# Cross-attention and a block-quantised feed-forward layer on one core: layer-norm scalings and the block-rounding additions moved from VectorE to GpSimd, with the rounding of 1024 columns cut into two halves

## The chip, the cores and the metric

The kernel runs on one core of a Trainium2 chip. The metric is the device time of one execution in microseconds (us). A core has several engines, each of which works through its own queue of instructions in order: TensorE (PE in the profile; its weight loads are shown apart as PEld), VectorE (DVE), ScalarE (ACT), GpSimd (POOL) and SyncE (SP), which issues most DMA transfers. Engines wait for each other through semaphores. SBUF is the on-chip memory, PSUM the small memory into which TensorE writes its products.

## The reference

There are B = 4 batches of N = 1024 rows of width 256, and 77 rows of context per batch. Cut to what matters:

```
# attention: 16 heads of width 16; keys are the 77 context rows and then the 1024 own rows
xn   = layernorm(x)
q    = xn @ Wq
k, v = split(concat(ctx, xn) @ Wkv)
dots = q k^T * 16 ** -0.5, causal over the own keys
x    = x + softmax(dots) v @ Wout + bout

# feed-forward: 256 -> 1024 -> 256, both factors of each product rounded in blocks of 32
def block_quant(v):                       # 3 mantissa bits
    amax  = max(abs(v)) over blocks of 32 along the last axis
    scale = 2 ** (floor(log2(amax)) - 3)
    return round(v / scale) * scale
h = gelu(block_quant(layernorm(x)) @ block_quant(w_fc)^T + b_fc)
x = x + block_quant(h) @ block_quant(w_proj)^T + b_proj
```

The kernel rounds a block by adding a large number `mag`, made from the block's largest magnitude, and subtracting it again: the addition in 32-bit floating point drops the bits that are to go. So a rounding is a maximum per block, two small operations that make `mag`, an add and a subtract.

## The kernel before, in words

Rows are handled in tiles of 128: eight tiles (`it`) per batch, 32 in all (`t`).

**The main loop.** Attention is cut into 16 parts, counted by `kk`: four batches times four groups of four heads. Each `kk` has 14 pieces (a piece is a stretch of up to 512 queries against 128 keys), each done in two half-steps of two heads. `half_step` (L831) issues, for two heads, two matmuls for the running maximum of the *next* `kk` (L451, into the PSUM tiles `s_ps`) and two matmuls for the scores of this one (L515, into `st_ps`); then VectorE reduces the two maxima (a plain reduce at L475 or a masked one with a running maximum at L477), ScalarE takes the exponential into an SBUF tile `pt` (L526) and GpSimd sets the masked part of the diagonal pieces to zero in place (`affine_select`, L531). The product with the values, `times_v` (L552), is issued two steps later. PSUM has three buffers for `s_ps` and two for `st_ps`; there are six `pt`.

**Everything else is fitted between half-steps.** A "unit" is a list of stages. `run` (L849) holds a list of units for each `kk`, with a price for each, and after each half-step begins as many as its budget allows, if their `ready` conditions hold. A unit's first stage is issued at once; each later one is issued a number of ticks after the one before it (a tick is a half-step): `LATER = 3`, unless the stage is given with a number of its own, as `(1, rounding)` is. The units that this change touches or that stand beside them:

- `norm_unit` (L304): `scale_rows` (L311) applies the first layer norm to a tile, `xh = (xn - mean) * rstd`; three ticks later PE transposes it (L324) and ScalarE copies it out (L326). There are 32. The roots `rstd` are made by `inv_std` (L153 to L163), 14 small VectorE operations for four tiles. The eight tiles of the first batch are done before the main loop starts.
- `in_unit` (L667): `quantize` applies the second layer norm (L674) to a tile `xh` of 256 columns and rounds it to `xq` (`quant_steps`, L171 to L180, and `quant_round`, L191 and L192); three ticks later PE transposes `xq` (L683). There are 32.
- `hidden_unit` (L694): matmuls to 1024 columns and the gelu on ScalarE (L713), into one of four buffers `h`.
- `out_unit` (L721): `largest` makes `mag` for the 1024 columns of `h`; one tick later `rounding` adds and subtracts, into one of two buffers `hq`; three ticks later `turn` transposes (L736) and ScalarE copies (L739); three more later `project` multiplies (L744), adds to `x` (L748) and issues the output transfer. `done["round"]`, counted in `rounding`, tells when the `h` buffer is free for another `hidden_unit`.
- `weight_unit` (L756): fetches and rounds a 128 x 256 block of a feed-forward weight. There are 16, in the first four `kk`.
- `clear_units` (L246): sets buffers to constants, on GpSimd: `vaug` (L248, L254), `qT` (L250) and `kT` (L252). They are issued after the norms of the first batch.

The feed-forward layer of a batch runs between the half-steps of the next batch: `in_unit`s in its second `kk`, `out_unit`s in the third and fourth. The last batch has no next one: from about 1084 us on, its feed-forward units are issued tick after tick with nothing beside them.

Before the change, the two steps of a rounding are on two engines:

```
nc.vector.tensor_tensor(src3, src3, magb, ALU.add)
nc.gpsimd.tensor_tensor(
    dst.rearrange("p (n k) -> p n k", k=QBLK), src3, magb, ALU.subtract
)
```

Of the kernel before, what the change touches and what calls it, by code (L numbers as in the profile page):

```python
# [10 lines left out]
BF16 = mybir.dt.bfloat16  # L11
I32 = mybir.dt.int32
AF = mybir.ActivationFunctionType
ALU = mybir.AluOpType
# [3 lines left out]
P = 128  # L18
# [10 lines left out]
QBLK = 32  # L29
# [14 lines left out]
def kernel(  # L44
# [14 lines left out]
    nc = tc.nc  # L59
    B, N, D = x.shape  # L60
    M = mem.shape[1]
    HID = w_fc.shape[0]
# [102 lines left out]
    def quant_steps(src, n, tag):  # L165

        nb = n // QBLK
        amax = small.tile([P, nb], F32, name=f"amax{tag}")  # L170
        nc.vector.tensor_reduce(  # L171
            amax, src.rearrange("p (n k) -> p n k", k=QBLK), axis=AX.X, op=ALU.max,
            apply_absolute_value=True,
        )
        mag = small.tile([P, nb], F32, name=f"mag{tag}")
        nc.vector.tensor_scalar(
            mag.bitcast(I32), amax.bitcast(I32), 0x7F800000, 0x00400000,
            ALU.bitwise_and, ALU.bitwise_or,
        )
        nc.vector.tensor_scalar(  # L180
            mag, mag, 1.5 * 2.0 ** -126, 2.0 ** (23 - MBITS), ALU.max, ALU.mult
        )
        return mag

    def quant_round(src, mag, dst):


        n = src.shape[-1]
        magb = mag.unsqueeze(2).broadcast_to([P, n // QBLK, QBLK])
        src3 = src.rearrange("p (n k) -> p n k", k=QBLK)  # L190
        nc.vector.tensor_tensor(src3, src3, magb, ALU.add)  # L191
        nc.gpsimd.tensor_tensor(  # L192
            dst.rearrange("p (n k) -> p n k", k=QBLK), src3, magb, ALU.subtract
        )
# [8 lines left out]
    with ExitStack() as actx:  # L203
# [11 lines left out]
        ffn = ap("ffn", 2)  # L215
# [40 lines left out]
        def s_tile(shape, dtype=F32):  # L256
            return ps_s.tile(shape, dtype, tag="s", name="s_ps")
# [11 lines left out]
        def cost(us, unit):  # L269

            first = unit[0] if isinstance(unit, list) else unit
            first.cost = us
            return unit
# [5 lines left out]
        def room(tag, bufs):  # L279
            return lambda: held[tag] < bufs  # L280
# [23 lines left out]
        def norm_unit(b, it):  # L304
            t = b * NT + it
            got = {}

            def scale_rows():
                held["xh"] += 1
                xh = work.tile([P, D], F32, name="xh")  # L310
                nc.vector.tensor_scalar(  # L311
                    xh, xn[b, it // HN][:, it % HN, :], mv1[:, t, 0:1], rstd1[:, t : t + 1],
                    ALU.subtract, ALU.mult,
                )
                got["xh"] = xh

            def turn():
                if it == 0:

                    assert b == 0 or projected[b - 1] == 2 * KC  # L320
                    xT[b] = xtp.tile([P, KC, KEYS], F32, name="xT")
                tp = s_tile([P, KC, P])
                for k in range(KC):
                    nc.tensor.transpose(tp[:, k, :], got["xh"][:, k * P : (k + 1) * P], ident)  # L324
                held["xh"] -= 1
                nc.scalar.copy(xT[b][:, :, M + it * P : M + (it + 1) * P], tp)  # L326
                normed[b] += 1

            scale_rows.ready = room("xh", XH)
            return cost(0.8, [scale_rows, turn])  # L330
# [256 lines left out]
        done = {"out": 0, "round": 0, "wout": 0, "begun": 0}  # L587
# [70 lines left out]
        xqT, hs, rooted = {}, {}, set()  # L658
# [8 lines left out]
        def in_unit(t):  # L667
            got = {}

            def quantize():  # L670
                done["begun"] += 1
                held["xq"] += 1
                xh = work.tile([P, D], F32, name="xh")
                nc.vector.tensor_scalar(  # L674
                    xh, x2[t], mv2[:, t, 0:1], rstd2[:, t : t + 1], ALU.subtract, ALU.mult
                )
                got["xq"] = ffn.tile([P, D], BF16, name="xq", bufs=XQ)
                quant_round(xh, quant_steps(xh, D, "x"), got["xq"])

            def turn():  # L680
                tp = s_tile([P, KC, P], BF16)
                for k in range(KC):
                    nc.tensor.transpose(tp[:, k, :], got["xq"][:, k * P : (k + 1) * P], identb)  # L683
                held["xq"] -= 1
                xqT[t] = ffn.tile([P, KC, P], BF16, name="xqT", bufs=HBUF + 1)
                nc.scalar.copy(xqT[t], tp)  # L686

            quantize.ready = lambda: (
                t // HN in rooted and done["begun"] - len(hs) <= HBUF
                and held["xq"] < XQ and held["xh"] < XH  # L690
            )
            return cost(1.6, [quantize, turn])
# [28 lines left out]
        def out_unit(t):  # L721
            got = {}

            def largest():
                held["hq"] += 1
                got["mag"] = quant_steps(hs[t], HID, "h")

            def rounding():
                got["hq"] = ffn.tile([P, HID], BF16, name="hq")
                quant_round(hs[t], got["mag"], got["hq"])  # L730
                done["round"] += 1

            def turn():
                tp = s_tile([P, HC, P], BF16)
                for k in range(HC):
                    nc.tensor.transpose(tp[:, k, :], got["hq"][:, k * P : (k + 1) * P], identb)  # L736
                held["hq"] -= 1
                got["hT"] = ffn.tile([P, HC, P], BF16, name="hT")
                nc.scalar.copy(got["hT"], tp)  # L739

            def project():
                yp = s_tile([P, D])
                for k in range(HC):
                    nc.tensor.matmul(  # L744
                        yp, got["hT"][:, k, :], wprT[:, k, :], start=(k == 0), stop=False
                    )
                nc.tensor.matmul(yp, ones3, bias3[:, B_PROJ : B_PROJ + D], start=False, stop=True)  # L747
                nc.vector.tensor_add(x2[t], x2[t], yp)  # L748
                nc.sync.dma_start(out=of[t * P : (t + 1) * P, :], in_=x2[t])
                done["out"] += 1  # L750

            largest.ready = lambda: t in hs and held["hq"] < 2
            return cost(4.4, [largest, (1, rounding), turn, project])


        def weight_unit(src, into):  # L756
# [144 lines left out]
        for kk in range(last + 1):  # L901
# [26 lines left out]
            else:  # L928
                n = -(-len(w_units) // NG)
# [61 lines left out]
```

## Time and profile before

| | |
|---|---|
| time, median of 4 runs | 1172.04 us (1169.41 to 1177.0) |
| the profiled execution | 1173.21 us, of which the profile's span is 1171.5 us |
| PE busy | 1043.7 us, 89% of the span |
| DVE busy | 767.8 us, 66% |
| ACT busy | 515.9 us, 44% |
| POOL busy | 224.8 us, 19% |
| TensorE clock granted, mean | 0.90 of full speed |

How to read the lines. The page gives busy time of each engine with its share of the span and its number of instructions; then the span in 40 equal slices, one digit for each: the busy share of the slice in tenths, and for PEclk the TensorE clock that was granted, in tenths of full speed; then the chain of work that ended last, by engine. A line of a group of instructions has the code line, the engine, the operation, what it writes and reads with shapes, how often it ran; after the first bar the total busy time in us and the mean of one in ns; after the second bar the idle time of the engine just before these instructions, and who ended it. A line of the timeline has the start in us, the duration in us and the operation; in square brackets the wait before it and who ended it.

### The profile page before, as it was taken

What the parts mean: (1) busy time and instruction counts of PE and PEld (TensorE: products, weight loads), DVE (VectorE), ACT (ScalarE), POOL (GpSimd) and SP (SyncE); (2) the same over time, 40 slices, a digit from 0 to 9 for tenths busy, and PEclk for the clock granted to TensorE, in tenths of its full rate; (3) what the DMA queues carried; (4) which work ended last, traced back from release to release, by engine and by line L of the source; (5) the groups of instructions that cost most, each with busy time, mean ns of one, the idle gap of its engine ahead of it and who ended that gap; (6) DMA issues with size and microseconds to landing.
All of it is one profiled execution on the core that took longest, in us unless ns stands there. A gap on an engine that the chain in (4) does not pass through costs nothing.

```text
span 1171.5 us, 20970 instructions
## 1 busy us (share of the span) xinstructions
PE 1043.7 (89%) x8014; PEld 432.2 (37%) x8024; DVE 767.8 (66%) x2410; ACT 515.9 (44%) x720; POOL 224.8 (19%) x419
## 2 busy tenths in 40 slices
PE   2799999999998899999988899999999899998665
PEld 1353334343433234344433324434434234343222
DVE  8686876665676575567568756657667586652654
ACT  2133554555343344565424364555434454663212
POOL 3000212121101122122201112112211122141312
PEclk9887999999978689999979689999999898999565
DMA  2121001101310001100320001010111000002100
GB/s 75 39 67 25 18 26 36 39 16 37 98 36 14 6 1 35 35 7 29 93 51 13 14 7 30 16 25 22 49 46 43 6 12 11 16 22 64 31 13 18
DMA packets 36118, 36.35 MB, mean 31 GB/s; under 512 B 14005, under 2 KB 29679, under 8 KB 36018
## 3 DMA queue, kind: packets, MB, share of 16 engines
q1 hardware_dynamic: 34912, 33.95, 10.6%
q8 instruction: 63, 1.03, 0.4%
q10 hardware_dynamic: 1106, 1.07, 0.3%
q14 instruction: 37, 0.30, 0.1%
HBM read 16.59 MB, written 5.24 MB: 19 GB/s over the span
## 4 chain that ended last, share of the span: by engine, by line
PE 68%; DVE 22%; issue 3%; DMA 2%; ACT 2%; SPq 1%; POOL 1%; POOLq 0%; DVEq 0%; ACTq 0%
PE s_ps L451 30%; PE av_ps L552 13%; PE s_ps L386 5%; DVE jk L477 4%; PE st_ps L515 4%; PE st_ps L702 3%; DVE mx L475 3%; PE s_ps L642 3%; DVE amaxh L171 2%; PE s_ps L359 2%; PE st_ps L707 2%; PE s_ps L744 2%; DVE h L191 1%; PE s_ps L736 1%; DVE st L145 1%
## 5 line engine op out<-in xcount | busy, mean ns | idle before, releaser
L451 PE MATMUL s_ps<-kT,qT 32*128 32x512 f32 (+2 forms) x1736 | 530.9, 566 | 59.3 <-DVE mxp L477 26.5
L526 ACT ACTIVATE pt<-st_ps 128x1024 f32<-128x1024 f32 (+4 forms) x448 | 355.4, 795 | 417.5 <-PE st_ps L515 392.1
L515 PE MATMUL st_ps<-qT,kT 32*128 32x512 f32 (+5 forms) x1792 | 533.6, 562 | 0.2 <-ACT pt L526 0.2
L451 PEld LDWEIGHTS s_ps<-kT,qT 32*128 32x128 f32 x1736 | 205.6, 195 | 252.7 <-DVE mxp L477 72.1
L531 POOL TENSOR_SCALAR_AFFINE_SELECT pt<-pt 128x254 f32<-128x254 f32 (+3 forms) x320 | 123.7, 388 | 618.3 <-ACT pt L526 618.3
L477 DVE CUSTOM_DVE_ANT_0 jk<-s_ps,tri,mx 128x77 bf16<-128x77 f32 (+3 forms) x372 | 173.1, 505 | 98.1 <-PE st_ps L515 73.1
L552 PE MATMUL av_ps<-pt,vaug 128*32 128x256 f32 (+7 forms) x3072 | 230.6, 374 | 7.2 <-POOL pt L531 4.2
L475 DVE TENSOR_REDUCE mx<-s_ps 128x1 f32<-128x512 f32 x248 | 159.7, 685 | 117.2 <-PE st_ps L515 94.0
L515 PEld LDWEIGHTS st_ps<-qT,kT 32*128 32x128 f32 (+1 forms) x1792 | 202.1, 191 | 14.7 <-issue 9.2
L477 DVE CUSTOM_DVE_ANT_0 jk<-s_ps,tri 128x512 bf16<-128x512 f32 (+3 forms) x248 | 126.6, 549 | 62.3 <-PE st_ps L515 50.4
L552 PEld LDWEIGHTS av_ps<-pt,vaug 128*32 128x32 f32 (+1 forms) x3072 | 62.3, 110 | 216.5 <-issue 167.5
L192 POOL TENSOR_TENSOR hq<-h,magh 128x1024 bf16<-128x1024 f32 x32 | 61.2, 1913 | 185.4 <-DVE h L191 185.4
L393 ACT COPY qk_st<-s_ps 128x512 f32<-128x512 f32 (+1 forms) x40 | 20.4, 514 | 73.2 <-PE s_ps L386 66.8
L713 ACT ACTIVATE h<-st_ps 128x1024 f32<-128x1024 f32 x32 | 32.8, 1024 | 39.9 <-PE st_ps L707 39.7
L702 PE MATMUL st_ps<-wfcT,xqT 128*128 128x512 bf16 x118 | 46.6, 477 | 4.2 <-ACT xqT L686 3.1
L739 ACT COPY hT<-s_ps 128x1024 bf16<-128x1024 bf16 x32 | 32.4, 1011 | 36.0 <-PE s_ps L736 35.8
L748 DVE TENSOR_TENSOR x<-x,s_ps 128x256 f32<-128x256 f32 x32 | 13.3, 416 | 47.8 <-PE s_ps L747 47.8
L642 PE MATMUL s_ps<-wo_sb,o_pk 128*128 128x256 f32 x128 | 41.6, 452 | 1.9 <-DVE o_pk L620 1.6
L171 DVE TENSOR_REDUCE amaxh<-h 128x32 f32<-128x1024 f32 x32 | 38.6, 1208 | 5.7 <-ACT h L713 5.7
L477 DVE DVE_READ_ACCUMULATOR2_ANT mxp<- 128x1 f32 x512 | 42.2, 82 | 0.0
L744 PE MATMUL s_ps<-wprT,hT 128*128 128x256 bf16 x256 | 40.5, 311 | 1.2 <-ACT hT L739 1.2
L191 DVE TENSOR_TENSOR h<-h,magh 128x1024 f32<-128x1024 f32 x32 | 39.4, 1233 | 0.4
(90 smaller groups left out, 766.5 us busy)
## 6 DMA issues: line engine op xcount, KB each, us to landing
kT<-qk_st SPq DMA_DIRECT2D x16, 275.2 KB
xn<-in_x_dram SPq DMA_DIRECT2D x16, 256.0 KB
qT<-qk_st SPq DMA_DIRECT2D x16, 256.0 KB
o_pk<-o_st SPq DMA_DIRECT2D x32, 128.0 KB
rb<-rd SPq DMA_DIRECT2D x128, 32.0 KB
x<-in_x_dram SPq DMA_DIRECT2D x32, 128.0 KB
out_dram<-x SPq DMA_DIRECT2D x32, 128.0 KB
x<-in_L_ffn_w_fc_dram SPq DMA_DIRECT2D x8, 128.0 KB
```

What stands on the lines that cost most here:

```text
L171: nc.vector.tensor_reduce(amax, src.rearrange("p (n k) -> p n k", k=QBLK), axis=AX.X, op=ALU.max, apply_absolute_value=True,)
L192: nc.gpsimd.tensor_tensor(dst.rearrange("p (n k) -> p n k", k=QBLK), src3, magb, ALU.subtract)
L451: nc.tensor.matmul(sp[:, 0 : hi - lo], qTs[kk % NQK][rows, it * P : (it + 1) * P], kTs[kk % NQK][rows, lo:hi], start=True, stop=True,)
L475: nc.vector.tensor_reduce(into, sp[:, 0:w], axis=AX.X, op=ALU.max)
L477: nc.vector.tensor_tensor_reduce(junk.tile([P, ICW], BF16, name="jk")[:, 0:w], sp[:, 0:w], mask, 1.0, before, ALU.add, ALU.max, into)
L515: nc.tensor.matmul(st[:nj, e, : i1 - i0], kTs[kk % NQK][rows, t * P : t * P + nj], qTs[kk % NQK][rows, i0:i1], start=True, stop=True,)
L526: nc.scalar.activation(pt[:nj, :, :w], st[:nj, :, :w], AF.Exp, scale=scale)
L531: nc.gpsimd.affine_select(out=pt[:nj, :, :behind], in_=pt[:nj, :, :behind], compare_op=ALU.is_ge, fill=0.0, base=base, pattern=[[0, 2], [1 ...
L552: nc.tensor.matmul(acc[c * PAD : (c + 1) * PAD, off + lo : off + hi], vaugs[b % 2][:nj, t, v0 : v0 + PAD], pts[kk, n, c // 2][:nj, c % 2, ...
L642: nc.tensor.matmul(yp, o_pk[b, ic][:, k, it * P % ICW : it * P % ICW + P], wo_sb[:, k, :], start=(k == 0), stop=False,)
L702: nc.tensor.matmul(hp[:, n, :], xqT[t][:, k, :], wfcT[:, k, n * ICW : (n + 1) * ICW], start=(k == 0), stop=False,)
L744: nc.tensor.matmul(yp, got["hT"][:, k, :], wprT[:, k, :], start=(k == 0), stop=False)
```

## The change

Three things move from VectorE to GpSimd, and one stage is cut in two.

1. The add of every rounding (`quant_round`, L191): 48 of 128 x 256 and 32 of 128 x 1024. GpSimd then does the add and the subtract one after the other.
2. The first layer norm's scaling (`scale_rows`, L311): 32 of 128 x 256.
3. The second layer norm's scaling in `in_unit` (L674): 32 of 128 x 256.
4. The rounding of `h` in `out_unit` is done in two halves of 512 columns, the first one tick after `largest`, the second one tick after that. So `turn` comes five ticks after `largest` instead of four, and `done["round"]` is counted with the second half.

```diff
@@ quant_round
-        nc.vector.tensor_tensor(src3, src3, magb, ALU.add)
+        nc.gpsimd.tensor_tensor(src3, src3, magb, ALU.add)
         nc.gpsimd.tensor_tensor(
             dst.rearrange("p (n k) -> p n k", k=QBLK), src3, magb, ALU.subtract
         )
@@ norm_unit, scale_rows
-                nc.vector.tensor_scalar(
+                nc.gpsimd.tensor_scalar(
                     xh, xn[b, it // HN][:, it % HN, :], mv1[:, t, 0:1], rstd1[:, t : t + 1],
                     ALU.subtract, ALU.mult,
                 )
@@ in_unit, quantize
-                nc.vector.tensor_scalar(
+                nc.gpsimd.tensor_scalar(
                     xh, x2[t], mv2[:, t, 0:1], rstd2[:, t : t + 1], ALU.subtract, ALU.mult
                 )
@@ out_unit
-            def rounding():
-                got["hq"] = ffn.tile([P, HID], BF16, name="hq")
-                quant_round(hs[t], got["mag"], got["hq"])
-                done["round"] += 1
+            def rounding(part):
+                def emit():
+                    if part == 0:
+                        got["hq"] = ffn.tile([P, HID], BF16, name="hq")
+                    n = HID // 2
+                    cols = slice(part * n, (part + 1) * n)
+                    blocks = slice(part * n // QBLK, (part + 1) * n // QBLK)
+                    quant_round(hs[t][:, cols], got["mag"][:, blocks], got["hq"][:, cols])
+                    done["round"] += part
+                return emit
...
-            return cost(4.4, [largest, (1, rounding), turn, project])
+            return cost(4.4, [largest, (1, rounding(0)), (1, rounding(1)), turn, project])
```

## The prediction

> **What bounds the kernel now.** I read the page first: engine totals, slices, chain.
>
> ```profile
> span 1171.5 us, 20970 instructions
> PE 1043.7 (89%) x8014; PEld 432.2 (37%) x8024; DVE 767.8 (66%) x2410; ACT 515.9 (44%) x720; POOL 224.8 (19%) x419
> PE   2799999999998899999988899999999899998665
> PEclk9887999999978689999979689999999898999565
> PE 68%; DVE 22%; issue 3%; DMA 2%; ACT 2%; SPq 1%; POOL 1%; POOLq 0%; DVEq 0%; ACTq 0%
> ```
>
> PE bounds it: busy 89%, 68% of the chain. DVE is second (22%), POOL has four fifths of the span free. PE is slack only in the first slice and in the last three (29.3 us a slice). So DVE time taken away pays at the two ends, and in the middle only where PE waits for DVE. Windows of 60 us from 60 to 1080 us sum to PE 955.0 of 1020, so 65 us idle there. Reading them against the timeline, about 21 us of idleness lie in steady stretches, two thirds (14) ended by DVE; the rest is around the reciprocal roots (L153 to L163), which stay as they are.
>
> Then the groups by shape, for the instructions that move:
>
> ```profile
> L191 DVE TENSOR_TENSOR h<-h,magh 128x1024 f32<-128x1024 f32 x32 | 39.4, 1233 | 0.4
> L191 DVE TENSOR_TENSOR xh<-xh,magx 128x256 f32<-128x256 f32 x32 | 13.6, 425 | 1.1
> L674 DVE TENSOR_SCALAR xh<-x,mv,rstd 128x256 f32<-128x256 f32 x32 | 13.4, 420 | 0.1
> L192 POOL TENSOR_TENSOR hq<-h,magh 128x1024 bf16<-128x1024 f32 x32 | 61.2, 1913 | 185.4 <-DVE h L191 185.4
> L531 POOL TENSOR_SCALAR_AFFINE_SELECT pt<-pt 128x254 f32<-128x254 f32 x192 | 83.9, 437 | 227.4 <-ACT pt L526 227.4
> ```
>
> The last column matters: POOL's subtract waited for DVE's add; POOL's mask waits for ACT's exponential. After the change, norms and adds stand in the same in-order queue as that mask.
>
> Last the timeline, where DVE and POOL touch each other:
>
> ```profile
> 6.95 5.49 DVE L153 TENSOR_SCALAR v<-mv 128x4 f32<-128x4 f32 x1
> 12.47 0.17 DVE L155 TENSOR_SCALAR y<-v 128x4 int32<-128x4 int32 x1
> ...
> 7.25 1.09 POOL L252 COPY kT<-negrow 128x1101 f32<-128x1101 f32 x1
> 10.22 2.19 POOL L254 MEMSET vaug<- 128x2520 f32 x1
> ```
>
> A four-element operation took 5.49 us and ended (12.44) with POOL's last clear (10.22 + 2.19 = 12.41); its like take 0.17. Reductions next to POOL work (L171, L475) show no such stretch.
>
> The Trainium skill, "SBUF — State Buffer", section "Who interferes with whom", says that the two engines share one port pair as an exclusive lock held for a whole instruction, and that reductions never take it. This trace agrees in both halves; by the rule, each added microsecond of POOL is one in which a DVE scalar operation may be shut out.
>
> **The change part by part.** DVE loses 32 adds of 1.233, 48 of 0.425, 32 L674 of 0.420 and 32 L311 of 0.419: 39.4 + 20.4 + 13.4 + 12.6 = 85.8 us, 768 to 682. POOL gains them. From the two subtract shapes (643 ns for 256 columns, 1913 for 1024) a column costs 1.65 ns, so 512 cost 0.643 + 256 x 0.00165 = 1.07. The new adds read and write as much; I price them like subtracts. 128 halves x 1.07 = 137 instead of 61.2; 48 adds x 0.64 = 31; 64 norms of which POOL shows no example: between 0.27 (a clear of 2520 columns at 2.19, scaled to 256, with 0.05 of start) and 0.64 (the subtract), taken 0.45 as the mask of 254 columns (0.437): 29. POOL goes to about 360 us, 31%: not a bound on average. What it costs must come from order.
>
> *Start.* L311's first eight operations now stand in POOL's queue ahead of six clears (L248 to L254, 4.21 to 12.41 us), which are issued after them. So POOL waits for the root and L153 is not shut out: the root is ready near 9.7 instead of 15.0, and the chain there (L153 5.50) loses 5.3. The clears move to about 17 to 25.4, and DVE's bias casts, a stretch of 12.2 us (22.79 to 35.04), may be shut out by them: 25.4 + 12.2 = 37.6. The first maximum, at 42.81 after 7.76 of idleness, would like to start at 37.5. So -5; bounds 0 (casts or transfers hold it) and -6.5.
>
> *Weights and norms of the middle.* 16 adds and 24 L311: 6.8 + 10.1 = 16.9 us off DVE, in stretches where PE waits little for it, and a POOL norm is three half-steps ahead of its transpose. -3; bounds 0 and -6.
>
> *Rounding of the hidden tiles.* 24 adds of 1.23 leave DVE in the middle = 29.6 us, 19 of which the chain from 60 to 1060 us names; but PE is idle for only some 14 us because of DVE, and other DVE work (maxima L477 and L475, L171) comes next at once. -5; bounds 0 and -14. Each transpose, projection, ACT copy L739 and output transfer on SP's queue goes one half-step (about 2.3 us) later, and the hidden unit that needs the freed tile too. I cost that at nothing: PE has scores and maxima of the same half-step to run; with no cover, which is the tail, it is below. A mask on POOL may stand behind an add and a subtract, 2.1 us instead of 1.9: covered by the two steps before its product L552.
>
> *Rounding of the normed tiles, 24 in the middle.* Before: L674, L171, two L176/L180, L191 on DVE without a break, 1.65 us (433.66 to 435.31). After: POOL norm, DVE largest and magnitude (0.85), POOL add, POOL subtract. DVE is spared 0.8, but waits: the norm stands behind the previous subtract and behind a mask that waits for ACT. While DVE waits at L171, the next half-step's maxima stand behind it, and PE waits for them through the three PSUM buffers. POOL per unit and half-step: mask 0.44 + norm 0.45 + add 0.64 + subtract 0.64 = 2.17, plus 0.85 of DVE in between = 3.05 with the hand-offs partly overlapped; a half-step is 2.3 (448 of them in some 1040 us). In bursts of four, the first loses nothing and the slack of a PSUM buffer takes most of the second. +0.25 a unit, +6; bounds 0 and 24 x 1.2 = +29.
>
> *The last batch, 1084 to 1171 us, nothing beside it.*
>
> ```profile
> 1099.48 1.91 POOL L192 TENSOR_TENSOR hq<-h,magh 128x1024 bf16<-128x1024 f32 x1 [2.53 <-DVE h L191]
> 1100.68 0.75 DVE L176 TENSOR_SCALAR magh<-amaxh 128x32 int32<-128x32 int32 x1
> 1101.45 1.03 PE L736 MATMUL s_ps<-identb,hq 128*128 128x128 bf16 x8 [2.22 <-POOL hq L192]
> ```
>
> PE waits for POOL. DVE add and POOL subtract ran as two stages (1.23, 1.91); now POOL does both, 4 x 1.07 = 4.3 us a tile against 3.6 apart in the trace. Working the schedule through: third tile rounded at 1111.9 (1105.0 before), since the fourth tile's norm now comes first; the second root at 1132 (1128.2), as L153 is shut out by POOL's halves; the colder PE (clock 0.50 to 0.62 there) catches some up. +4; bounds 0 and +8.
>
> The Trainium skill, "GPSIMD Engine Reference", section 4.1 "Engine selection", speaks against the change: two-input elementwise work belongs on VectorE, GpSimd being about 2x slower. This trace has 643 against 425 ns and 1913 against 1233, 1.5x; at 2x a half add would take 1.23 instead of 1.07, some 2.6 us more over the eight tiles of the tail.
>
> Sum: -5 - 3 - 5 + 6 + 4 = -3. The profiled execution took 1173.21 (span 1171.5 + 1.71 around), so 1170.2; the median shown is 1172.04, so 1169.
>
> **Rivals.**
> 1. *The round trip decides (slower).* Place: the bursts of normed tiles where DVE runs without a break (424 to 439, 697 to 710, 911 to 925 us). Each costs the full 3.05 - 2.3 = 0.75: 24 x 0.75 = +18 instead of +6, so +9, 1181. It makes the kernel measurably slower from (6 + 8.9) / 24 = 0.62 a unit. For it: the 227.4 us that POOL waits for ACT, in front of every norm. Against: the first of a burst and the half-steps without a mask are free.
> 2. *DVE's relief pays in full.* The 14 us of DVE-ended idleness go and the round trip hides: -5 - 3 - 14 + 0 + 4 = -18, 1154. For it: DVE 22% of the chain, where L191 has 19 us. Against: PE is at 28 to 29.5 of 30 us in most windows, so the gain ends early.
> 3. *The relief frees only idle DVE time and the start gain is lost to the casts*: 0 + 0 + 0 + 0 + 4, 1176.
>
> **How the numbers follow.** A change of 0.5% (5.9 us) is about what a measurement can tell from none: the same lies from 1166.2 to 1177.9. The sum as worked has 0.36, with its own range 1162 to 1177; rival 1 0.34; rival 2 0.26; rival 3 0.04. Faster: all of rival 2 and 0.14 of the first, 0.40. Same: 0.20 of the first and 0.03, 0.23. Slower: 0.37. All lower bounds together give -26.5 (1145), all upper ones +37 (1209); all at once is unlikely. 1150 to 1190 leaves out about 0.06 of rival 2 and 0.11 of rival 1, where waits also cool PE's clock (it went to 0.53 from 390 to 420 us after one).
>
> **What would show it.** Right: DVE near 682 and POOL near 360 us; the first L153 at 0.2 and the first maximum 5 us earlier; POOL halves at 1.07; L171 of the normed tiles with idle time released by POOL's norm, below 1 us each; the second root of the last batch after 1130. Rival 1: PE waits at L451 for DVE grow by over 10 us, with L171 behind POOL. Rival 2: they shrink by as much. Wrong altogether if a POOL norm takes far from 0.45, if POOL's instructions slow one another or DVE's by the shared access more than the 0.2 to 1.4 us seen at L176, or if PE's clock turns out differently in the phases after the roots.

## The result

The changed kernel is slower: 1182.9 us (median of 44 runs) against 1173.6 us for the kernel before (70 runs), a ratio of 1.0073 with a 95% interval of 1.0055 to 1.0091. (Here and below, ratios leave out the executions that lay more than 1.5% above the fastest of their kernel, so they differ a little from the quotient of the medians.) The forecast was 1169, a little faster and within what a measurement can tell; the time lies inside the stated range and within 2 us of the first rival. As the experiments show, that nearness to the rival is luck: two terms of the sum were wrong by some 30 and 40 us, with opposite signs.

The page of the changed kernel, the same parts that were shown of before (span, busy time, PE's slices, the granted clock, the chain by engine):

```profile
span 1185.1 us, 21024 instructions
PE 1053.7 (89%) x8015; PEld 437.7 (37%) x8024; DVE 687.4 (58%) x2266; ACT 515.5 (44%) x720; POOL 403.8 (34%) x627
PE   3799999999897989999988889999998999995666
PEclk9887999999897779999977788999998879988565
PE 69%; DVE 14%; POOL 8%; issue 4%; ACT 2%; DMA 2%; SPq 0%; POOLq 0%; ACTq 0%; DVEq 0%
```

DVE has become as light as forecast (687 us, forecast 682) and its share of the chain fell from 22% to 14%. POOL took 8% of the chain, and 404 us instead of the forecast 360. The groups by shape say where the 44 us more come from:

```profile
L191 POOL TENSOR_TENSOR h<-h,magh 128x512 f32<-128x512 f32 x64 | 67.5, 1055 | 105.5 <-DVE magh L180 61.9 <-ACT pt L526 40.0 <-PE s_ps L753 3.6
L191 POOL TENSOR_TENSOR xh<-xh,magx 128x256 f32<-128x256 f32 x32 | 19.7, 616 | 41.6 <-DVE magx L180 41.6
L311 POOL TENSOR_SCALAR xh<-xn,mv,rstd 128x256 f32<-128x256 f32 x32 | 41.5, 1304 | 29.6 <-DVE rstd L163 29.6
L674 POOL TENSOR_SCALAR xh<-x,mv,rstd 128x256 f32<-128x256 f32 x32 | 39.1, 1222 | 15.6 <-DVE rstd L163 15.6
L171 DVE TENSOR_REDUCE amaxx<-xh 128x8 f32<-128x256 f32 x32 | 13.4, 419 | 66.7 <-POOL xh L674 66.7
```

The adds cost what was forecast (1.055 us for a half, forecast 1.07; 0.616 for 256 columns, forecast 0.64). A norm on POOL takes 1.22 us (all 32 of L674 lie between 1.219 and 1.226; the mean of L311, 1.30, holds a few of up to 2.13, but its median is 1.22 too), where 0.45 was taken and 0.64 was the upper bound; on DVE it took 0.42. And DVE's search for the largest (L171) has waited 66.7 us for it, over 2 us for each tile.

To see where the time went, both traces are cut at the same places of the work. L485 (a transpose of the maxima) runs 32 times in every kernel; the 12th, 14th, 20th, 22nd, 28th and 30th of them enclose the three stretches in which the normed tiles of a batch are rounded, and after the 32nd comes the end with the last batch. Windows of before at these places (start and end, length, PE, PEld, DVE, ACT and POOL busy, granted clock, share of DMA, GB/s):

```profile
367.91:455.15 87.24, 80.72 (x514) 29.63 (x517) 52.72 (x174) 37.47 (x55) 15.10 (x30) 0.77 0.06 15
645.11:727.38 82.27, 75.67 (x514) 29.46 (x517) 53.01 (x172) 37.34 (x55) 15.09 (x30) 0.82 0.06 16
906.91:975.71 68.80, 59.32 (x483) 22.76 (x484) 50.15 (x167) 33.82 (x46) 15.07 (x30) 0.92 0.02 8
1030.53:1171.50 140.97, 101.66 (x606) 43.20 (x608) 70.32 (x156) 45.84 (x59) 37.29 (x40) 0.71 0.10 31
```

The same windows of the changed kernel:

```profile
362.46:450.93 88.47, 78.58 (x512) 30.50 (x517) 42.80 (x152) 37.01 (x55) 36.52 (x53) 0.77 0.06 15
640.01:729.91 89.90, 80.45 (x512) 31.63 (x517) 42.91 (x152) 36.81 (x55) 36.52 (x53) 0.76 0.05 15
904.88:979.91 75.03, 66.75 (x481) 25.40 (x484) 41.89 (x147) 33.52 (x46) 31.69 (x50) 0.80 0.02 7
1030.55:1185.10 154.55, 109.62 (x613) 45.64 (x616) 48.43 (x129) 47.04 (x60) 77.58 (x92) 0.67 0.09 28
```

DVE has 10 us less to do in each stretch, and yet the stretches did not become shorter: 253.4 us together instead of 238.3. The end is 13.6 us longer. The rest gained: 5.4 us up to the first stretch (362.5 instead of 367.9) and 9.6 between the stretches (414.7 instead of 424.3). 15.09 + 13.58 - 5.45 - 9.62 = 13.60, the difference of the two spans.

### The profile page after: what moved, and what is told of

It is laid out like the page before. It is cut to its first block, busy times and chain, and to the rows that moved or that the text cites. A ratio compares the mean times of both kernels' runs of the same rounds, so it can differ in the third digit from the quotient of the medians.

```text
span 1185.1 us, 21024 instructions
## 1 busy us (share of the span) xinstructions
PE 1053.7 (89%) x8015; PEld 437.7 (37%) x8024; DVE 687.4 (58%) x2266; ACT 515.5 (44%) x720; POOL 403.8 (34%) x627
## 3 DMA queue, kind: packets, MB, share of 16 engines
q10 hardware_dynamic: 1106, 1.07, 0.3%
## 4 chain that ended last, share of the span: by engine, by line
PE 69%; DVE 14%; POOL 8%; issue 4%; ACT 2%; DMA 2%; SPq 0%; POOLq 0%; ACTq 0%; DVEq 0%
PE s_ps L451 30%; PE av_ps L552 14%; PE s_ps L386 6%; PE st_ps L515 5%; POOL xh L674 3%; PE s_ps L750 3%; PE st_ps L702 3%; PE s_ps L642 2%; PE s_ps L359 2%; DVE jk L477 2%; DVE mx L475 2%; DVE amaxh L171 2%; PE st_ps L707 2%; DVE amaxx L171 1%; DVE st L145 1%
## 5 line engine op out<-in xcount | busy, mean ns | idle before, releaser
L451 PE MATMUL s_ps<-kT,qT 32*128 32x512 f32 (+2 forms) x1736 | 532.2, 570 | 61.1 <-DVE mxp L477 26.5
L451 PEld LDWEIGHTS s_ps<-kT,qT 32*128 32x128 f32 x1736 | 208.0, 197 | 254.5 <-DVE mxp L477 72.9
L531 POOL TENSOR_SCALAR_AFFINE_SELECT pt<-pt 128x254 f32<-128x254 f32 (+3 forms) x320 | 121.0, 380 | 524.2 <-ACT pt L526 524.0
L552 PE MATMUL av_ps<-pt,vaug 128*32 128x256 f32 (+7 forms) x3072 | 236.9, 383 | 3.8 <-ACT o_st L574 1.3
L477 DVE CUSTOM_DVE_ANT_0 jk<-s_ps,tri,mx 128x77 bf16<-128x77 f32 (+3 forms) x372 | 173.9, 505 | 105.5 <-PE st_ps L515 78.4
L515 PEld LDWEIGHTS st_ps<-qT,kT 32*128 32x128 f32 (+1 forms) x1792 | 204.6, 195 | 16.3 <-issue 8.9
L477 DVE CUSTOM_DVE_ANT_0 jk<-s_ps,tri 128x512 bf16<-128x512 f32 (+3 forms) x248 | 126.3, 550 | 67.7 <-PE st_ps L515 53.8
L191 POOL TENSOR_TENSOR h<-h,magh 128x512 f32<-128x512 f32 x64 | 67.5, 1055 | 105.5 <-DVE magh L180 61.9
L192 POOL TENSOR_TENSOR hq<-h,magh 128x512 bf16<-128x512 f32 x64 | 67.5, 1054 | 5.0
L171 DVE TENSOR_REDUCE amaxx<-xh 128x8 f32<-128x256 f32 x32 | 13.4, 419 | 66.7 <-POOL xh L674 66.7
L311 POOL TENSOR_SCALAR xh<-xn,mv,rstd 128x256 f32<-128x256 f32 x32 | 41.5, 1304 | 29.6 <-DVE rstd L163 29.6
L713 ACT ACTIVATE h<-st_ps 128x1024 f32<-128x1024 f32 x32 | 32.7, 1024 | 35.4 <-PE st_ps L707 35.3
L702 PE MATMUL st_ps<-wfcT,xqT 128*128 128x512 bf16 x119 | 43.6, 447 | 2.8 <-ACT xqT L686 1.4
L674 POOL TENSOR_SCALAR xh<-x,mv,rstd 128x256 f32<-128x256 f32 x32 | 39.1, 1222 | 15.6 <-DVE rstd L163 15.6
```

What stands on the lines that cost most here:

```text
L191: nc.gpsimd.tensor_tensor(src3, src3, magb, ALU.add)
L451: nc.tensor.matmul(sp[:, 0 : hi - lo], qTs[kk % NQK][rows, it * P : (it + 1) * P], kTs[kk % NQK][rows, lo:hi], start=True, stop=True,)
L477: nc.vector.tensor_tensor_reduce(junk.tile([P, ICW], BF16, name="jk")[:, 0:w], sp[:, 0:w], mask, 1.0, before, ALU.add, ALU.max, into)
L515: nc.tensor.matmul(st[:nj, e, : i1 - i0], kTs[kk % NQK][rows, t * P : t * P + nj], qTs[kk % NQK][rows, i0:i1], start=True, stop=True,)
L531: nc.gpsimd.affine_select(out=pt[:nj, :, :behind], in_=pt[:nj, :, :behind], compare_op=ALU.is_ge, fill=0.0, base=base, pattern=[[0, 2], [1 ...
L552: nc.tensor.matmul(acc[c * PAD : (c + 1) * PAD, off + lo : off + hi], vaugs[b % 2][:nj, t, v0 : v0 + PAD], pts[kk, n, c // 2][:nj, c % 2, ...
```

## The experiments

Ratios are to the kernel before, measured on the same chip beside it, with 95% intervals. Times of stretches are from one profiled execution each; executions of one kernel differ by several us, as the granted clock does, so a few us in one stretch of one execution prove nothing. How far this goes can be read from two kernels below that differ from the one before only at the start (those with the clears held back): the same three stretches took 231.5 and 240.4 us in them, the end 139.4 and 139.9.

### The adds without the norms, and the norms without the adds

The first three runs part the change. Both norms back on VectorE:

```diff
-                nc.gpsimd.tensor_scalar(
+                nc.vector.tensor_scalar(
                     xh, xn[b, it // HN][:, it % HN, :], mv1[:, t, 0:1], rstd1[:, t : t + 1],
...
-                nc.gpsimd.tensor_scalar(
+                nc.vector.tensor_scalar(
                     xh, x2[t], mv2[:, t, 0:1], rstd2[:, t : t + 1], ALU.subtract, ALU.mult
```

> The changed kernel with both layer-norm scalings (L311, L674) back on VectorE; the adds stay on GpSimd and the 1024 columns stay in halves. Theory 1 (a GpSimd norm takes 1.22 to 1.30 us instead of the 0.45 that was assumed, and VectorE waits for each before it can look for the largest): the loss goes with the norms. The pace of the normed tiles in the last batch falls from 3.53 us to about 1.7, the part after the first root of the last batch shrinks by some 4 us, and the time is 0.992 to 1.000 of before. Rival (add and subtract one after the other on GpSimd, 4.2 us a tile, and the later transpose cost it): still slower than before, 1.005 or more.

Measured: 0.9665 (0.9635 to 0.9696), 1133.7 us. Far better than expected by either theory: the adds alone are worth 39 us.

The kernel before with the same two lines the other way round (`nc.vector` to `nc.gpsimd`) and nothing else:

> The kernel before with only the two layer-norm scalings moved to GpSimd; adds stay on VectorE, the rounding is not cut. Theory 1: slower than before, 1.006 to 1.015, with VectorE's L171 waiting over 2 us a tile for GpSimd's norm. Rival (the adds cost it): 0.997 to 1.003.

Measured: 1.0161 (1.0123 to 1.0200): slower, as theory 1 said, and by slightly more than its range. L171 waited 47.9 us for POOL, 1.5 a tile and not over 2.

The changed kernel with only the second of the two lines back on VectorE:

> The changed kernel with only the second norm's scaling (L674) back on VectorE; the first norm's (L311) stays on GpSimd. It parts the two norms: if the wait inside the rounding of the normed tiles is what costs, this gains nearly all that taking both back gains (0.993 to 1.001 of before); if the first norm on GpSimd costs as much (its eight at the start took 11.5 us, and the transposes of the later batches wait for it), it stays at 1.003 or above.

Measured: 0.9668 (0.9640 to 0.9696), the same as with both back. So the first norm on GpSimd costs nothing that can be told, although it takes 1.30 us on average there and the transposes wait for it now and then. The second norm in its place costs all: from 0.9668 to 1.0073, 47 us for 32 instructions of 1.22 us.

The stretches of the kernel with adds only:

```profile
362.09:437.67 75.58, 69.60 (x512) 28.19 (x517) 48.42 (x162) 36.76 (x55) 22.43 (x41) 0.90 0.07 18
626.98:703.44 76.46, 70.51 (x512) 28.23 (x517) 48.38 (x164) 36.76 (x55) 22.46 (x41) 0.89 0.07 17
879.22:941.81 62.59, 55.74 (x481) 22.18 (x484) 45.12 (x157) 33.52 (x46) 22.98 (x42) 0.95 0.03 9
992.52:1136.20 143.68, 107.42 (x613) 45.42 (x614) 53.47 (x137) 46.86 (x60) 67.70 (x84) 0.69 0.10 30
```

The three stretches take 214.6 us instead of 238.3. PE's busy time in them falls from 215.7 to 195.9 us, with the same matmuls: 20 of the 24 us gained are matmuls that run at a higher clock (0.90, 0.89 and 0.95 instead of 0.77, 0.82 and 0.92): busy time times clock is nearly the same, 62, 62 and 55 us before and 63, 63 and 53 here.

One execution of one stretch would not show this. With VectorE loaded as before, the first stretch once took 78.1 us at a clock of 0.89 (the kernel of "The start" with a copy of the roots), against 87.2 at 0.77 before. But the three stretches together took 231.5 to 240.4 us in the traces of this kernel, the one before and the one with the clears held back until the transposes, and 211.5 to 218.7 in all eight kernels in which VectorE has less to do for a normed tile and does not wait for GpSimd's norm at once.

### Is it the wait or GpSimd's time? The norm ahead

The changed kernel, with the second norm still on GpSimd, but as a stage of its own two ticks before the rest of its unit:

```diff
-            def quantize():
+            def norm():
                 done["begun"] += 1
                 held["xq"] += 1
-                xh = work.tile([P, D], F32, name="xh")
+                held["xh"] += 1
+                got["xh"] = xh = work.tile([P, D], F32, name="xh")
                 nc.gpsimd.tensor_scalar(
                     xh, x2[t], mv2[:, t, 0:1], rstd2[:, t : t + 1], ALU.subtract, ALU.mult
                 )
+
+            def quantize():
+                xh = got["xh"]
                 got["xq"] = ffn.tile([P, D], BF16, name="xq", bufs=XQ)
                 quant_round(xh, quant_steps(xh, D, "x"), got["xq"])
+                held["xh"] -= 1
...
-            return cost(1.6, [quantize, turn])
+            return cost(1.6, [norm, (2, quantize), turn])
```

> The changed kernel, with the second norm's scaling (L674) still on GpSimd but as a stage of its own, two ticks ahead of the look for the largest. GpSimd's work is the same; VectorE should find the norm done. If the wait of VectorE at L171 is what the second norm costs: L171's idle time falls from 66.7 us to below 25 and the time is 0.960 to 0.975 of before. If it is the GpSimd time itself (39 us in 32 instructions, in front of masks and roundings, or access shared with VectorE): 0.995 or above.

Measured: 0.9660 (0.9616 to 0.9703). GpSimd is as busy as with the change (401.9 us), the norm as long (1219 ns), and all of the loss is gone. It is VectorE's wait. The group by shape of this kernel:

```profile
L675 POOL TENSOR_SCALAR xh<-x,mv,rstd 128x256 f32<-128x256 f32 x32 | 39.0, 1219 | 15.3 <-DVE rstd L163 15.3
L171 DVE TENSOR_REDUCE amaxx<-xh 128x8 f32<-128x256 f32 x32 | 13.2, 414 | 15.4 <-POOL xh L675 15.4
```

66.7 us of waiting have become 15.4. What such a wait looked like with the change, in the timeline of the first stretch:

```profile
425.85 0.92 PE L451 MATMUL s_ps<-kT,qT 32*128 32x333 f32 x1
...
426.38 1.22 POOL L674 TENSOR_SCALAR xh<-x,mv,rstd 128x256 f32<-128x256 f32 x1
428.62 0.62 POOL L191 TENSOR_TENSOR xh<-xh,magx 128x256 f32<-128x256 f32 x1 [1.01 <-DVE magx L180]
429.31 0.62 POOL L192 TENSOR_TENSOR xq<-xh,magx 128x256 bf16<-128x256 f32 x1
429.88 0.42 POOL L531 TENSOR_SCALAR_AFFINE_SELECT pt<-pt 128x254 f32<-128x254 f32 x1
430.28 1.23 POOL L674 TENSOR_SCALAR xh<-x,mv,rstd 128x256 f32<-128x256 f32 x1
...
427.64 0.42 DVE L171 TENSOR_REDUCE amaxx<-xh 128x8 f32<-128x256 f32 x1 [1.84 <-POOL xh L674]
428.38 0.56 DVE L477 CUSTOM_DVE_ANT_0 jk<-s_ps,tri,mx 128x333 bf16<-128x333 f32 x1
```

From norm to norm 3.90 us pass. DVE stands idle for 1.84 of them, and the maxima of the next half-step (L477) stand behind L171 in its queue: PE had ended the matmul for the first of them at 426.77, and it ran at 428.38. Before, a tile took 2.6 to 2.9 us here:

```profile
432.66 0.62 POOL L192 TENSOR_TENSOR xq<-xh,magx 128x256 bf16<-128x256 f32 x1 [1.89 <-DVE xh L191]
435.54 0.62 POOL L192 TENSOR_TENSOR xq<-xh,magx 128x256 bf16<-128x256 f32 x1 [1.90 <-DVE xh L191]
438.17 0.62 POOL L192 TENSOR_TENSOR xq<-xh,magx 128x256 bf16<-128x256 f32 x1 [1.64 <-DVE xh L191]
```

On PE this shows twice, as idle time and as a lower clock. Windows around the second four tiles of the first stretch, first of before, then of the changed kernel (columns as above):

```profile
427.50:440.00 12.50, 10.88 (x97) 4.80 (x93) 11.56 (x40) 5.80 (x8) 4.58 (x11) 1.00 0.00 1
418.50:437.50 19.00, 14.75 (x94) 6.25 (x87) 8.30 (x32) 5.45 (x8) 11.74 (x18) 0.64 0.00 1
```

The kernel before ran 97 matmuls in 12.5 us at the full clock, the changed one 94 in 19.0, and from 424.0 to 437.5 us its clock was 0.50. The clock fell to 0.50 or 0.51 at this place in all three traces in which L171 waits for GpSimd's norm in this way (the changed kernel, the norms without the adds, the norm with constants).

### Why a norm takes 1.22 us on GpSimd

The changed kernel with two constants in place of each row's mean and reciprocal root, which leaves out the second layer norm:

```diff
-                    xh, x2[t], mv2[:, t, 0:1], rstd2[:, t : t + 1], ALU.subtract, ALU.mult
+                    xh, x2[t], 0.0, 1.0, ALU.subtract, ALU.mult
```

> The changed kernel with the second norm's scaling on GpSimd given two constants in place of the mean and the reciprocal root of each row; the second layer norm is left out of the computation. If reading the two values of each row is what makes this instruction take 1.22 us: 0.3 to 0.5 us, VectorE's wait at L171 falls to some 1 us a tile and the time is 0.975 to 0.995 of before. If it takes 1.2 us with constants too, the time is as with the change, 1.003 to 1.011.

Measured: 1.0009 (0.9970 to 1.0049). This is some 7 us better than the change and a little below what was expected for this case, but the first idea falls: with constants the instruction still takes 1.07 us.

```profile
L674 POOL TENSOR_SCALAR xh<-x 128x256 f32<-128x256 f32 x32 | 34.2, 1069 | 7.2 <-DVE x L647 7.2
```

The two values of each row cost 0.15 us; the rest comes with this kind of instruction on GpSimd. It is not the other engines' doing: with the rows' values all 32 took 1.219 to 1.226 us, wherever they stood. L171 still waited 59.3 us, and the three stretches of this execution took 256.1 us, no less than with the change.

### What the adds are worth, and which

Norms on VectorE; only the 32 adds of 1024 columns on GpSimd, in halves. `quant_round` gets the engine as an argument (shortened):

```diff
-        nc.gpsimd.tensor_tensor(src3, src3, magb, ALU.add)
+        (adder or nc.vector).tensor_tensor(src3, src3, magb, ALU.add)
...
-                    quant_round(hs[t][:, cols], got["mag"][:, blocks], got["hq"][:, cols])
+                    quant_round(hs[t][:, cols], got["mag"][:, blocks], got["hq"][:, cols], nc.gpsimd)
```

> Norms on VectorE, the 48 small adds on VectorE too; only the 32 adds of the 1024 columns are on GpSimd, in halves. They are 39.4 of the 59.8 us that the adds take from VectorE. If VectorE's relief pays in proportion to the time taken from it, 0.972 to 0.982 of before; if the small adds count most, because they stand in the bursts of normed tiles and of weights, 0.985 or above; if the large ones count alone, 0.962 to 0.970.

Measured: 0.9906 (0.9865 to 0.9948). 39.4 us less on VectorE bring 11 us: the second of the three expectations, that the small adds count most.

The kernel before with `nc.gpsimd` as that argument in `in_unit` alone (the 32 adds of normed tiles):

> The kernel before with only the 32 adds of the normed tiles (0.425 us each) on GpSimd; all else as before. If the small adds' worth lies in the three stretches with normed tiles: 0.975 to 0.985 of before, with those stretches some 20 us shorter and the granted clock there near 0.9. If it needs the large adds gone as well: 0.990 or above.

Measured: 0.9868 (0.9822 to 0.9914): 13.6 us less on VectorE bring some 15, a little less than the first expectation, with what it said of the stretches. The three stretches of its trace take 218.5 us, 20 less than before, at a granted clock of 0.89, 0.90 and 0.92.

The same in `weight_unit` alone:

> The kernel before with only the 16 adds of the weights on GpSimd. From the first 368 us of the runs with and without them (5.8 against 0.8 us gained): 0.994 to 0.998 of before. 1.000 if that difference was chance.

Measured: 0.9964 (0.9921 to 1.0007), some 4 us, not safely told from none.

The three ratios together give 0.9906 x 0.9868 x 0.9964 = 0.974, all adds at once 0.9665; the difference is about what the three intervals allow.

All adds on GpSimd, but the 1024 columns in one piece, one tick after the largest (`rounding` is again that of the kernel before):

```diff
-            return cost(4.4, [largest, (1, rounding(0)), (1, rounding(1)), turn, project])
+            return cost(4.4, [largest, (1, rounding), turn, project])
```

> All adds on GpSimd, norms on VectorE, but the 1024 columns rounded in one piece one tick after the largest, as before. If the two halves and the later transpose have no part in the gain: 0.962 to 0.971 of before, as with halves. If the gain comes from them (masks not held up by a rounding of 3.8 us, or the later transpose leaving PE its order): 0.975 or above.

Measured: 0.9804 (0.9756 to 0.9852): the halves, with the later transpose that comes with them, are worth 1.4%. In its trace the stretches are as short as with halves (215.2 against 214.6 us); the end is 154.7 us instead of 143.7. So what the halves save is, in these two executions, in the last batch: from the last exponential of the main loop on, 108.0 us in one piece, 98.9 in halves.

### VectorE's time or the hand-over?

The second norm left out, so that VectorE has 0.42 us less in each unit and GpSimd nothing new: the add reads `x` and writes the tile that the norm would have written (shortened; `quant_round` gets that tile as an argument).

```diff
-                nc.vector.tensor_scalar(
-                    xh, x2[t], mv2[:, t, 0:1], rstd2[:, t : t + 1], ALU.subtract, ALU.mult
-                )
...
-                quant_round(xh, quant_steps(xh, D, "x"), got["xq"])
+                quant_round(x2[t], quant_steps(x2[t], D, "x"), got["xq"], xh)
```

> The kernel before without the second norm's scaling (the normed tiles are rounded from x itself, so the second layer norm is left out of the computation); the add reads x and writes the same tile as before. VectorE loses 0.42 us a unit, as with the small adds moved, and GpSimd gets nothing. If VectorE's time in these units is what counts: the same ratio as with only their adds on GpSimd, within 0.006. If the hand-over counts (GpSimd doing add and subtract itself): 0.993 or above.

Measured: 0.9833 (0.9777 to 0.9888), within 0.006 of the 0.9868 with only the adds moved; its stretches take 218.7 us against 218.5. So a hand-over is not what brings the gain; VectorE's time in these units is.

Both steps together (the argument `nc.gpsimd` added in the last line of that diff):

> As the run without the second norm, and the adds of the normed tiles on GpSimd too (the second layer norm is left out): VectorE loses 0.85 us a unit. If its worth goes on in proportion: twice the gain of the single steps, 0.950 to 0.970. If PE is the bound once one of them is gone: hardly more than one step, 0.970 to 0.985.

Measured: 0.9851 (0.9798 to 0.9904). Twice the relief brings no more than one step, as the second expectation had it: the worth is a step, not a slope. What sets the pace once a unit is 0.4 us shorter on VectorE was not shown; the stretches of this trace took 212.1 us, 6 less than with one step, but its end was longer (146.8 us against 141.3).

Adding time instead of taking it. The kernel before with one more add of 256 columns on VectorE in each of the 32 units of normed tiles:

```diff
+                nc.vector.tensor_tensor(extra, x2[t], x2[t], ALU.add)
                 got["xq"] = ffn.tile([P, D], BF16, name="xq", bufs=XQ)
```

> The kernel before with one more VectorE add of 128 x 256 (0.43 us, result unused) in each of the 32 rounding units of normed tiles: 13.6 us more VectorE time in the places from which the change took the small adds. If VectorE time there is paid for several times over, because PE's clock falls and stays down: 1.007 or more of before, and a lower granted clock than 0.77, 0.82 and 0.92 in the three stretches with normed tiles. If VectorE time costs its share of the chain (22%, 3 us): 1.001 to 1.004.

Measured: 1.0062 (1.0028 to 1.0096): 13.6 us more on VectorE cost 7. The granted clock in the three stretches of its trace was 0.86, 0.82 and 0.88, one higher, one equal and one lower than before, and the stretches took 236.2 us together, no longer than before; the expectation of a lower clock fails.

The same add in the last stage of the out units:

> The same 32 adds of 0.43 us, but in the last stage of the out units, between maxima of the parts that have no normed tiles. If it is the place that makes VectorE time dear: 0.999 to 1.004 of before. If it is VectorE time as such: the same as with the adds in the normed tiles' units.

Measured: 1.0050 (1.0007 to 1.0092). The two cannot be told apart, so added VectorE time costs about half of itself in either place.

### The start

The kernel before, with a copy of the first roots ahead of the clears, so that these wait for the roots:

```diff
+        late_mark = small.tile([P, NT], F32, name="late")
+        nc.gpsimd.tensor_copy(late_mark, rstd1[:, 0:NT])
         run(-1, clear_units()[:1] + k_units(1) + v_units(0) + clear_units()[1:])
```

> The kernel before with one small GpSimd copy of the first roots put ahead of the six clears, so that these run after the roots. It measures the start by itself: the first root operation 0.17 us instead of 5.49, the first maximum 5 us earlier, the time 0.995 to 0.997 of before. If something else holds the start (transfers, or the bias casts which the clears now shut out), the first maximum comes less than 2 us earlier and the time stays within 0.998 to 1.002.

Measured: 0.9990 (0.9960 to 1.0020). Lines of its timeline, DVE and POOL:

```profile
7.07 0.17 DVE L153 TENSOR_SCALAR v<-mv 128x4 f32<-128x4 f32 x1
...
16.28 6.55 DVE L311 TENSOR_SCALAR xh<-xn,mv,rstd 128x256 f32<-128x256 f32 x4
...
16.36 2.20 POOL L248 MEMSET vaug<- 128x2520 f32 x1
```

The first root was free, as foreseen (0.17 us instead of 5.49). But the clears now began at 16.36, among the norms of the second four tiles, and these four took 6.55 us instead of the 1.38 of before. The first maximum came at 42.59, 0.2 earlier. The shut-out had only moved. So the clears were held back further, until the norms had been transposed:

```diff
+        late_mark = small.tile([P, KC], F32, name="late")
+        nc.gpsimd.tensor_copy(late_mark, xT[0][:, :, KEYS - 1])
         run(-1, clear_units()[:1] + k_units(1) + v_units(0) + clear_units()[1:])
```

> The kernel before with the six GpSimd clears held back until the first batch's norms have been transposed (a copy of four of their values stands ahead of the clears). It prices the start without VectorE's norms meeting the clears, which the copy of the roots did not. If the shut-out of the first root was worth what the prediction took: the first maximum 4 to 6 us earlier than 42.8 and 0.994 to 0.997 of before. If the bias casts, now next to the clears, hold it: less than 2 us and 0.998 to 1.002.

Measured: 0.9972 (0.9935 to 1.0009). The first maximum came at 38.68 us, 4.1 earlier than before, with the bias casts lengthened by the clears (one of 512 columns took 1.93 us instead of 0.41) but still done at 33.8. In the whole time it is on the edge of what can be told.

### Everything together

All adds on GpSimd in halves, the second norm there two ticks ahead, the first norm on VectorE, and the clears held back:

> All adds on GpSimd in halves, the second norm's scaling on GpSimd two ticks ahead, the first norm's on VectorE, and the clears held back. If the parts add up: 0.966 with the norm ahead, less 4 us at the start, 0.960 to 0.966 of before. If the start is held by something else, 0.964 to 0.970.

Measured: 0.9612 (0.9560 to 0.9663), 1126.2 us. This beats both kernels, the one before by 3.9% and the changed one by 4.6%. It fits the first expectation; from the 0.9660 with the norm ahead alone it cannot be told apart.

## Why the prediction was wrong, point by point

**What bounds the kernel.** "PE bounds it ... so 65 us idle there", and of these 14 to be had from DVE. This is the step that failed on the side of the gain. PE's busy time was read as time that the work needs. In the stretches with normed tiles it was not: PE was busy 215.7 of 238.3 us, but at a granted clock of 0.77 to 0.92, and with the adds on GpSimd the same matmuls took 195.9. The clock row was shown in the prediction (the two 6s of its middle stand in the first two stretches), but no term for the middle priced it; the prediction speaks of the clock in the last batch, at the edge of its range ("waits also cool PE's clock") and as a sign of being wrong.

**VectorE's relief.** Taken at -5 for the large adds, -3 for weights and first norms, and nothing separate for the small adds of normed tiles. Measured by themselves: large adds -0.9%, adds of normed tiles -1.3%, adds of weights -0.4%; all adds together with the halves -3.35%, 39 us (the start and the last batch included). The terms held 8 us (and 0.8 a unit inside the round trip) for what measured 39.

**The norm on GpSimd.** "Between 0.27 ... and 0.64, taken 0.45 as the mask of 254 columns": measured 1.22. Value and bounds came from other kinds of instruction (a clear, a mask, an add of two tensors) that have as many columns, and number of columns was the wrong likeness. The Trainium skill, "GPSIMD Engine Reference", section 4.1 "Engine selection", has operations with one input on GpSimd at roughly line rate. If that is read as VectorE's rate, it would have been about 0.42 us, an estimate from that page and the row of L674. The runs differ from it, 1.07 us with constants and 1.22 with the row's values, and the runs decide.

**The round trip.** "DVE is spared 0.8, but waits ... +0.25 a unit, +6; bounds 0 and ... +29." The mechanism was named rightly, down to the maxima standing behind L171. Its size was not: 47 us between the kernels with the second norm on VectorE and on GpSimd. Of the two reasons, one is the 1.22 us: with it in place of 0.45 the prediction's own sum for a unit is 3.82 us instead of 3.05, and 3.9 was measured. Where no half-step is free that is 24 x (3.82 - 2.3) = +36 by the prediction's formula, an estimate. The other is again the clock: with the wait, the stretches stayed at 0.77, 0.76 and 0.80 and none of the adds' relief (24 us there) could show. On the kernel before, where there was no relief to lose, both norms cost only 1.6%, 19 us.

**Rival 1** had this place and this sign, and its 1181 is close to the 1182.9 measured. But it reached it with -9 and +18; the runs show -39 and +47. Its sign in the profile, "PE waits at L451 for DVE grow by over 10 us", did not appear either (26.5 us for L477's result before and after): the loss shows as a colder PE and a waiting L171, not as waits at L451.

**Start.** "So -5": the first L153 took 0.17 us as foreseen, but the eight norms on POOL took 11.5 us (4.84 and 6.63 for four each) and the first maximum came 1.2 us earlier (41.62). The prediction's reason itself was sound: freed in another way, the start gave 4.1 us.

**The last batch.** "+4; bounds 0 and +8". The end grew by 13.6 us in one execution of each, but 6.3 of these lie before the last exponential of the main loop (39.9 us before, 46.2 after); from there on it is 101.1 against 108.4, +7.3, within the bounds. The kernels that leave this part as it was took 99.5 and 95.5 us there, so the size is not safe. POOL did work on a large tile for 4.2 us and the second root came after 1130, as stated (L153 at 1134.99, shut out for 0.97). What was missed is the pace of the normed tiles there, 3.53 us instead of 1.65, and that the last part of the main loop before it ran 20 us at a clock of 0.74 and 0.57. With the second norm back on VectorE the end took 137.0 us, and 143.7 with both back.

**Right:** the prices of adds and subtracts, DVE's total, the freed first root, the tick's delay of the transpose being harmless in the middle (with and without halves the stretches took 214.6 and 215.2 us, and the parts between them, where most of the large tiles are rounded, 415.8 and 415.9), and the port's shut-outs being small: L176 on the large tiles took 222 ns on average after the change, 276 before.

## What to carry to other kernels

Price a moved operation from a row of the same kind of instruction on the new engine; if there is none, let the bound be wide, since the number of columns says little. An operation that is handed to another engine's queue and awaited at once stops everything behind the wait: started two steps ahead, the same 1.22 us instruction turned 1.0073 into 0.966. And before calling TensorE the bound, read its busy time beside its clock: busy at three quarters of the clock can hide room, here 20 us of 216.

## What had not been expected of the hardware

- One GpSimd operation of the kind `(x - a) * b` on 128 x 256 took 1.22 us, twice the 0.62 of an add of two tensors of that size and 2.8 times the mask of 254 columns (0.43). With constants for `a` and `b` it took 1.07.
- TensorE's clock can stay low while TensorE is busy. A window of before, right after a pause at a root:

```profile
390.00:420.00 30.00, 29.38 (x119) 7.58 (x116) 11.09 (x25) 14.46 (x17) 2.05 (x4) 0.53 0.02 6
```

  PE was busy 29.4 of 30 us and had 0.53 of its clock. The Trainium skill, "TensorE: Matmul & The Clock Gate", section "What's actually happening", has the full clock come back after about 3.4 us of sustained work; this window does not agree, if the profile's busy time is such work. In the kernel with adds only the clock stood at 0.51 for 7 us around the same pause (380.5 to 387.5 us) and was whole from 388 on. What brings it back earlier there was not settled. Less VectorE time goes with it in four kernels (adds only, adds of normed tiles only, second norm left out, norm ahead), but adding VectorE time did not lower it further, and in one execution with VectorE loaded as before (the copy of the roots) it was back after 10.5 us, while with the adds and the first norm moved it took 17.
- The shut-out of VectorE by GpSimd's clears moves with the clears: made free at the first root, it met the norms (four took 6.55 us instead of 1.38), and held back from these, it met the bias casts.
